# Four background tiles become six, loaded in halves, and side work is tied to its place in the list

## The chip, the cores and the metric

The kernel runs on one core of one Trainium2 chip (trn2). The metric is the device time of the program in microseconds (us), as the median of several runs; lower is better.

## The reference

A graph network of four layers on N = 2708 nodes with D = 512 features, all in float32. Only the first two layers matter here.

```python
deg = jnp.maximum((adj != 0).astype(jnp.float32).sum(-1), 1.0)
# layer 0
x = layernorm(x + (adj + head(adj)) @ x / rowsum(adj + head(adj)))
# layer 1: attention on the mask of adj, and a plain product with adj
h = x @ W_sa;  s_left = h @ a_sa[0, :512];  s_right = h @ a_sa[0, 512:]
e = where(adj != 0, exp(-leaky_relu(s_left[:, None] + s_right[None, :], 0.01)), 0)
x_a = (e / (sum(e, axis=1) + 1e-5)) @ h
x_b = adj @ (x @ W_gcnb) + b_gcnb
attn_a, attn_b = sigmoid([adj @ x, x] @ Wa.T + ba), sigmoid([adj @ x, x] @ Wb.T + bb)
x = layernorm(x + sigmoid(attn_a * x_a + attn_b * x_b))
# layer 2: three products with adj in a row; layer 3: adj + I, scaled by deg ** -0.5 on both sides
```

`deg`, the count of non-zero entries in each row, is used by the last layer.

## The kernel before

**Tiling.** The host hands in the transposed adjacency `adjT`. Nodes are split in two halves of NH = 1354, so `adjT` has four quarters, named 11, 12, 21 and 22. A product of adjacency and features is done by a scheme with seven instead of eight block products, P1 to P7. It needs sums and differences of the quarters: s1 = 21 + 22, s3 = 11 - 21, s2 = s1 - 11, s4 = 12 - s2. A `sweep` takes one range of output columns after the other; in each range the seven products run one after the other on TensorE (PE), each over ten tiles of 128 rows, and the rest of the rows (KR = 74 of each half) is added by small matmuls. [...]

**Stages.** `S` gives the start of each stage in units of one product of a sweep: S[0] = 0 is layer 0, S[1] = 28 a sweep with the plain adjacency over one range (1024, 330), S[2] = 35 the attention sweep over four ranges of 384, 384, 256 and 330 columns, SB = 63 the plain adjacency for the other 1024 columns by two nested levels of the scheme (`sweep2`), and S[3] to S[6] layers 2 and 3.

**Order.** Nothing is issued directly. `at(pos, fn, hold)` puts a piece of work into a list at a position in those units. The list is sorted, and the functions are called in its order. The framework then places the instructions on the engines by that order and by when they would be ready, so an instruction can be placed ahead of one that is earlier in the list if that one is not ready yet. With `hold=True` each instruction of the piece gets an ordering edge, without a semaphore, from the instruction ahead of it in the list on its engine: it can't be placed before that one. At run time every engine works in the order that was placed.

**Around the attention sweep.** In a range that starts at position pb, the tiles 11, 21, 22 and 12 of `adjT` come through SP's queue into a ring of 38 buffers. `prep2` (L1143 to L1145) makes each tile into e: two ACT operations (Prelu, Exp) and one on VectorE (DVE). `comb` (L407) makes the sums on DVE. `add_run` (L766 to L770) adds tiles up on DVE, and `run_sums` (matmul L783) turns the sum into row sums on PE, for h = 1 at pb + 4.7 and h = 0 at pb + 5.2. Their reciprocals `rd` (L1156, L1157) scale the output rows as these leave PSUM (`done2`, matmul L610, ACT L1198), from pb + 5.15 and pb + 7.12.

**Background.** During S[2], the sums s1 to s4 of the other 1024 columns are made and written to DRAM (`SD`, "As" in the profile) for SB, and their counts are taken for `deg`. There are two sets of 512 columns (`RANGES_B`), each with ten steps and a step for the rest of the rows. In a step, `back_load` loads four tiles of 128 x 512 (L1059, 256 KB each, on the GpSimd (POOL) queue); `back_tally` takes Sign twice and Square once per pair of tiles on ACT (L1072, L1073) and adds to `dg` on DVE (L1075); `back_sums` makes the four sums in place on DVE (L1095) and stores each (L1096, POOL queue). The four tiles `w_0` to `w_3` have one buffer each. After a set, `back_end` (matmul L1103) makes the degrees and `back_rows` stores them as a row.

**In S[1].** `score` (L907) takes dot products of each feature row with the attention vectors on DVE, `scores_end` collects them, and `score_rows` turns them over with PE (`to_rows`, L924) into a row in DRAM that S[2] reads. Two of the four products are taken for 16 of the tiles in S[2]. `pair` in `extra1` (ACT L973, L974; DVE L980) counts the columns of S[1]'s own range, and `end` there (L993) sums them on PE.

Of the kernel before, what the change touches and what calls it, by code (L numbers as in the profile page):

```python
# [21 lines left out]
F32 = mybir.dt.float32  # L22
# [3 lines left out]
P = 128  # L26
EPS = 1e-5
NH = 1354
# [43 lines left out]
def gnn_kernel(ctx: ExitStack, tc: tile.TileContext, x, adjT, w_sa, a_sa, w_gcn, b_gcn, wab, bab, w_hop, w_out,  # L72
# [873 lines left out]
    for R0, n in RANGES:  # L946
        full = R0 == RANGES_A[0][0]
        for h in (1, 0):
            ts = tiles_of(R0, n)
            for k in ts:  # L950
                p = S[1] + 0.55 + 0.21 * i
                at(p, lambda t=h * KT + k: get_x1(t))
                at(p + 0.25, lambda t=h * KT + k, w=wt(k), js=range(4 if full else 2): score(t, w, got1, js))
                i += 1
            at(p + 0.26, lambda a=(h * KT + ts[0], len(ts), False): scores_end(*a))
            if full:
                at(p + 0.26, lambda a=(h * KT + ts[0], len(ts), True): scores_end(*a))
            at(p + 0.8, lambda R0=R0, h=h, ts=ts: score_rows(R0, h, ts))
    at(p + 0.27, scores_over)
    for i, (h, k) in enumerate((h, k) for g in (4, 0) for h in (0, 1) for k in range(g, g + 4)):  # L960
        p = S[2] + 1.6 + 1.3 * i
        at(p, lambda t=h * KT + k: get_x1(t))
        at(p + 0.4, lambda t=h * KT + k: score(t, P, got1, (2, 3)))
        if k % 4 == 3:
            at(p + 0.41, lambda a=(h * KT + k - 3, 4, True): scores_end(*a))

    def extra1(pb, r, R0, n, A):
        ts = tiles_of(R0, n)

        def pair(keys, w=P):  # L970
            m = pool.tile([P, 2, D], BF, name="sg", tag="nat", bufs=6)
            for h, key in enumerate(keys):
                nc.scalar.activation(m[:w, h, :n], A[(r,) + key][:w, :n], AF.Sign)  # L973
            nc.scalar.activation(m[:w, :, :n], m[:w, :, :n], AF.Square)  # L974
            if R0 not in deg:
                deg[R0] = d = pool.tile([P, 2, D], BF, name="dg", tag="nat", bufs=6)
                nc.vector.tensor_copy(d[:w, :, :n], m[:w, :, :n])
            else:
                d = deg[R0]
                nc.vector.tensor_tensor(d[:w, :, :n], d[:w, :, :n], m[:w, :, :n], ALU.add)  # L980

        for k in range(KW):
            at(pb + 0.1 + 0.8 * k / KT, lambda k=k: pair((("11", k), ("21", k))))
            at(pb + 3.9 + 0.8 * k / KT, lambda k=k: pair((("12", k), ("22", k))))
        for key, w in (("r", KA), ("r32", 32)):
            at(pb + 4.8, lambda key=key, w=w: pair(((key, 0), (key, 1)), w))

        def end(h):
            d = deg[R0]
            ps = bank("ds", [P, 4])  # L990
            for i, q in enumerate(ts):
                wq = wt(q)
                nc.tensor.matmul(ps[:wq, i : i + 1], d[:, h, q * P - R0 : q * P - R0 + wq], ones_bf[:, 0:1], start=True,  # L993
                                 stop=True)
# [12 lines left out]
        at(pb + 5.9, lambda: rows(1))  # L1007
        at(pb + 5.2, lambda: end(0))
        at(pb + 5.9, lambda: rows(0))
# [37 lines left out]

    back = {}

    def back_tiles():  # L1050
        return [feat.tile([P, D], F32, name=f"bk_{c}", tag=f"w_{c}") for c in range(4)]

    QUARTERS = ((0, 0), (1, 0), (1, 1), (0, 1))

    def back_load(i0, k):
        back["t"] = ts = back_tiles()
        for t, (hi, hj) in zip(ts, QUARTERS):
            j0, c0 = hj * NH + k * P, hi * NH + i0
            nc.gpsimd.dma_start(out=t, in_=adjT[j0 : j0 + P, c0 : c0 + D])  # L1059

    def back_rest_load(i0):
        back["t"] = ts = back_tiles()
        for h in range(2):
            a = adjT[:, h * NH + i0 : h * NH + i0 + D]
            rows_over(nc.gpsimd, ts[h], (a[NH - KR : NH], a[2 * NH - KR :]))
            nc.gpsimd.dma_start(out=ts[2 + h][:32], in_=a[2 * NH - 32 :])

    def tally(pair, w):

        m = pool.tile([P, 2, D], BF, name="sg", tag="nat", bufs=6)  # L1070
        for h in range(2):
            nc.scalar.activation(m[:w, h, :], pair[h][:w], AF.Sign)  # L1072
        nc.scalar.activation(m[:w], m[:w], AF.Square)  # L1073
        d = back["d"]
        nc.vector.tensor_tensor(d[:w], d[:w], m[:w], ALU.add)  # L1075

    def back_start():
        back["d"] = pool.tile([P, 2, D], BF, name="dg", tag="nat", bufs=6)
        nc.gpsimd.memset(back["d"], 0.0)

    def back_tally():
        a11, a21, a22, a12 = back["t"]
        tally((a11, a21), P)
        tally((a12, a22), P)

    def back_rest_tally():
        ts = back["t"]
        tally(ts[:2], KA)
        tally(ts[2:], 32)

    def back_sums(i0, k):
        a11, a21, a22, a12 = back["t"]
        for m, o, a, b, op in (("s1", a22, a21, a22, ALU.add), ("s3", a21, a11, a21, ALU.subtract),
                               ("s2", a11, a22, a11, ALU.subtract), ("s4", a12, a12, a11, ALU.subtract)):
            nc.vector.tensor_tensor(o, a, b, op)  # L1095
            nc.gpsimd.dma_start(out=SD[m][k * P : (k + 1) * P, i0 : i0 + D], in_=o)  # L1096

    def back_end(i0):
        d = back.pop("d")
        ps = bank("ds", [P, 8])  # L1100
        for h in range(2):
            for i in range(4):
                nc.tensor.matmul(ps[:, 4 * h + i : 4 * h + i + 1], d[:, h, i * P : (i + 1) * P], ones_bf[:, 0:1], start=True,  # L1103
                                 stop=True)
# [8 lines left out]
        q = h * KT + i0 // P  # L1113
        to_rows(rdeg[:, q : q + 4], 4, DROW[h][0, i0 : i0 + D].rearrange("(k i) -> k i", i=P))

    p = S[2] + 1.3
    for i0, _ in RANGES_B:
        at(p, back_start)
        for k in range(KW):
            at(p, lambda i0=i0, k=k: back_load(i0, k))  # L1120
            at(p + 0.6, back_tally)
            at(p + 0.7, lambda i0=i0, k=k: back_sums(i0, k))
            p += 1.13
        at(p, lambda i0=i0: back_rest_load(i0))
        at(p + 0.6, back_rest_tally)
        at(p + 0.85, lambda i0=i0: back_end(i0))
        at(p + 0.9, lambda i0=i0: back_rows(i0, 0))
        at(p + 0.95, lambda i0=i0: back_rows(i0, 1))
        p += 1.13

    def start2b():
        W[2] = [spare_part(s, g) for s in ("T1", "T2", "T3", "T4") for g in "BD"]
# [14 lines left out]
    def extra2(pb, r, R0, n, A):  # L1147
        def rows(h):
            row[R0, h] = tmp("row")
            m = (n + P - 1) // P  # L1150
            src = SROW[R0, h][0:1, :]
            nc.sync.dma_start(out=row[R0, h][:, : m * P].rearrange("p (k i) -> p k i", i=P),
                              in_=bass.AP(tensor=src.tensor, offset=src.offset, ap=[[0, P], [P, m], [1, P]]))

        def share(o, s, t, w):
            nc.vector.tensor_scalar(o, s, 1e-5, None, ALU.add)  # L1156
            nc.vector.reciprocal(o, o)  # L1157
            if R0 == RANGES_A[0][0]:
                nc.vector.tensor_tensor(o, o, gate[:w, t, 0:1], ALU.mult)

        at(pb - 1.6, lambda: rows(0))
        at(pb - 1.0, lambda: rows(1))
        at(pb + 5.2, lambda: run_sums(R0, n, 0, share))
        at(pb + 4.7, lambda: run_sums(R0, n, 1, share))

    def finish_x2(y, x1, w, t, h, r0):

# [608 lines left out]
```

## Time and profile before

| | |
|---|---|
| median of 3 runs | 2927.16 us (2924.32 to 2930.38) |
| the profiled execution | 2930.68 us |
| its span, first to last instruction | 2928.9 us |
| mean granted TensorE clock | 0.988 |
| PE / DVE / ACT / POOL busy | 97% / 78% / 23% / 22% of the span |
| data moved | 554.41 MB, 189 GB/s |
| `bk<-in_adjT` loads (L1059) | 80 of 256 KB, 4.6 us from issue to landing (median) |
| `As<-bk` stores (L1096) | 80 of 256 KB, 3.2 us (median) |

PE is the TensorE matmul, PEld its weight loads, DVE VectorE, ACT ScalarE, POOL GpSimd, SP SyncE. A row such as `L1095 DVE bk<-bk,bk` names the line, the engine and what is written from what. In the list of waits, `PE rs L783 <- DVE run L770` says that PE stood idle ahead of the instruction of line 783 that writes rs, until DVE's instruction of line 770 that writes run had ended. The profile's windows give for a stretch of time the busy time of each engine with the count of instructions, then the granted clock of TensorE, the busy share of the DMA engines and GB/s.

### The profile page before, as it was taken

How to read it: one execution, taken by the hardware profiler on the slowest of the kernel's cores; microseconds unless marked ns; L12 is line 12 of the kernel's file. 1: busy time of each engine (PE TensorE's matmuls, PEld its weight loads, DVE VectorE, ACT ScalarE, POOL GpSimd, SP SyncE). 2: the span in 40 equal slices, each digit the busy share in tenths (PEclk: the TensorE clock that was granted, in tenths of full speed). 3: DMA queues.
4: the chain of work that ended last, by engine and by line, in shares of the span. 5: the costliest groups of instructions: out<-in, count | busy, mean ns of one | idle time of the engine just before them, and what ended most of it. 6: DMA issues, size and time to landing. Idle time of an engine off the chain costs nothing.

```text
span 2928.9 us, 38864 instructions
## 1 busy us (share of the span) xinstructions
PE 2832.2 (97%) x11159; PEld 1913.9 (65%) x11159; DVE 2292.8 (78%) x5890; ACT 661.3 (23%) x1314; POOL 650.8 (22%) x1175
## 2 busy tenths in 40 slices
PE   7999999999989899999999999999999999999998
PEld 5655666556576678777666666666666666656665
DVE  6898688676667657677599877987878877899986
ACT  4554214765557311201200000000000100100001
POOL 0123233222232210213202224021230221501102
PEclk9999999999999999999999999999999999999999
DMA  7666466466566565577767768566675565854652
GB/s 225 194 204 186 140 206 205 138 206 190 168 203 197 164 183 146 176 221 244 228 177 240 211 196 257 166 184 213 192 251 165 177 202 176 251 152 138 182 140 79
DMA packets 404959, 554.41 MB, mean 189 GB/s; under 512 B 68752, under 2 KB 350556, under 8 KB 404744
## 3 DMA queue, kind: packets, MB, share of 16 engines
q1 hardware_dynamic: 330976, 391.33, 45.8%
q0 software_dynamic: 56032, 148.83, 15.4%
q10 hardware_dynamic: 17736, 11.76, 1.4%
q8 instruction: 89, 1.46, 0.2%
q14 instruction: 126, 1.03, 0.1%
HBM read 468.02 MB, written 83.65 MB: 188 GB/s over the span
## 4 chain that ended last, share of the span: by engine, by line
PE 71%; DVE 12%; issue 6%; DMA 6%; POOL 3%; ACT 1%; SPq 1%; POOLq 0%; DVEq 0%; ACTq 0%
PE accd L1356 13%; PE accu L1356 13%; PE accc L1356 12%; PE ps_d L610 6%; PE acca L1356 6%; PE accd L462 4%; PE accc L462 3%; PE accr L1427 3%; PE accu L462 3%; DMA bk<-in_adjT 2%; PE acca L462 2%; DVE z L1301 2%; DMA As<-bk 1%; PE accr L1431 1%; PE ps L649 1%
## 5 line engine op out<-in xcount | busy, mean ns | idle before, releaser
L1301 DVE TENSOR_TENSOR z<-z 128x339 f32<-128x339 f32 (+2 forms) x1176 | 538.4, 490 | 20.4 <-PE accu L1356 10.6
L1374 ACT COPY q<-accu 128x339 f32<-128x339 f32 (+2 forms) x105 | 41.6, 429 | 1056.7 <-PE accu L1356 836.2
L1356 PE MATMUL accc<-s,t 128*128 128x339 f32 (+2 forms) x784 | 233.5, 439 | 0.2 <-DVE s L1301 0.2
L1356 PE MATMUL accu<-z,t 128*128 128x339 f32 (+2 forms) x784 | 227.7, 436 | 4.2 <-DVE z L1301 3.0
L1356 PE MATMUL accd<-z,t 128*128 128x339 f32 (+2 forms) x784 | 227.8, 436 | 1.7 <-DVE q L1438 1.4
L1356 PE MATMUL accc<-z,t 128*128 128x339 f32 (+2 forms) x784 | 226.8, 436 | 0.5 <-ACT q L1374 0.5
L564 POOL TENSOR_TENSOR rstd<-rstd,neg_half 128x1 f32<-128x1 f32 (+3 forms) x91 | 59.7, 656 | 702.0 <-DVE rstd L563 446.9
L1356 PEld LDWEIGHTS accu<-z,t 128*128 128x128 f32 x784 | 148.1, 190 | 70.1 <-DVE z L1301 6.1
L1356 PEld LDWEIGHTS accc<-s,t 128*128 128x128 f32 x784 | 146.8, 190 | 70.7 <-issue 10.2
L1356 PEld LDWEIGHTS accd<-z,t 128*128 128x128 f32 x784 | 148.1, 190 | 66.7 <-DVE q L1438 2.3
L1356 PEld LDWEIGHTS accc<-z,t 128*128 128x128 f32 x784 | 148.2, 190 | 64.8 <-ACT q L1374 1.0
L1380 DVE TENSOR_TENSOR q<-q,accd 128x338 f32<-128x338 f32 (+2 forms) x140 | 67.9, 485 | 148.3 <-PE accd L1356 148.0
L1301 DVE TENSOR_TENSOR s<-z 128x339 f32<-128x339 f32 (+2 forms) x392 | 178.0, 490 | 7.5 <-PE accc L1356 3.2
L1575 POOL DMA_DIRECT2D Y<-y x192 | 104.7, 552 | 330.0 <-DVE y L1570 289.2
L407 DVE TENSOR_TENSOR a<-a,a 128x384 f32<-128x384 f32 (+2 forms) x240 | 118.0, 516 | 5.3 <-DMA a<-in_adjT 4.3
L1143 ACT ACTIVATE e<-row,s_right 128x384 f32<-128x384 f32 (+5 forms) x176 | 94.8, 566 | 41.0 <-DVE a L1145 11.6
L1145 DVE SCALAR_TENSOR_TENSOR a<-a,e 128x384 f32<-128x384 f32 (+2 forms) x160 | 76.9, 508 | 34.1 <-ACT e L1144 34.0
L569 ACT ACTIVATE ld<-ld,rstd 128x512 f32<-128x512 f32 (+3 forms) x45 | 36.5, 813 | 263.9 <-DVE rstd L566 98.1
L1438 DVE TENSOR_TENSOR q<-q,accr 128x338 f32<-128x338 f32 (+2 forms) x160 | 69.1, 485 | 22.8 <-PE accr L1431 22.7
L1380 DVE TENSOR_TENSOR q<-q,accu 128x338 f32<-128x338 f32 (+2 forms) x175 | 79.2, 485 | 3.9 <-ACT q L1374 2.6
L774 DVE SCALAR_TENSOR_TENSOR s<-a,row 128x384 f32<-128x384 f32 (+2 forms) x152 | 75.3, 508 | 6.0 <-ACT row L759 6.0
L1144 ACT ACTIVATE e<-e 128x384 f32<-128x384 f32 (+5 forms) x176 | 78.9, 475 | 1.4
(699 smaller groups left out, 5907.5 us busy)
## 6 DMA issues: line engine op xcount, KB each, us to landing
z<-As SPq DMA_DIRECT2D x320, 169.5 KB
z<-As SPq DMA_DIRECT2D x320, 169.0 KB
z<-in_adjT SPq DMA_DIRECT2D x240, 169.5 KB
z<-in_adjT SPq DMA_DIRECT2D x240, 169.0 KB
a<-in_adjT SPq DMA_DIRECT2D x160, 192.0 KB
bk<-in_adjT POOLq DMA_DIRECT2D x80, 256.0 KB, 4.6
As<-bk POOLq DMA_DIRECT2D x80, 256.0 KB, 3.2
z<-As SPq DMA_DIRECT2D x160, 128.0 KB
```

The source lines that it names most:

```text
L407: nc.vector.tensor_tensor(A[r, dst, k][:, :n], A[r, a, k][:, :n], A[r, b, k][:, :n], op)
L462: nc.tensor.matmul(B[home, c][:, :n], X[STAT[p], k][:, c * P : (c + 1) * P], A[r, MOV[p], k][:, :n], start=bool(start and k == k0), stop=k ...
L610: nc.tensor.matmul(o, lhs(c), r, start=c == 0 and n == 0, stop=c == DC - 1, skip_group_check=True)
L774: nc.vector.scalar_tensor_tensor(t[:w, :n], a[:w, :n], 0.0, row[R0, h][:w, :n], ALU.is_gt, ALU.mult)
L1143: nc.scalar.activation(e[:w, :n], row[R0, h][:w, :n], AF.Prelu, bias=s_right[:w, t : t + 1], alpha=0.01)
L1144: nc.scalar.activation(e[:w, :n], e[:w, :n], AF.Exp, scale=-1.0)
L1145: nc.vector.scalar_tensor_tensor(a[:w, :n], a[:w, :n], 0.0, e[:w, :n], ALU.not_equal, ALU.mult)
L1301: nc.vector.tensor_tensor(d[:, :n], Z[x + (k,)][:, :n], Z[y + (k,)][:, :n], op)
L1356: nc.tensor.matmul(B[home][:, :n], stat(v, k), a[:, :n], start=bool(start and k == 0), stop=k == nk - 1, skip_group_check=True)
L1380: nc.vector.tensor_tensor(d[:, :n], s_[:, :n], B[home][:, :n], ALU.add)
L1427: nc.tensor.matmul(ps[r][:, :n], XA[:KA, c * P : (c + 1) * P], R[h, s][:KA, :n], start=True, stop=False, skip_group_check=True)
L1575: nc.gpsimd.dma_start(out=rows[:, :, f * P : (f + 1) * P], in_=o[32 * f : 32 * (f + 1), : m * P].rearrange("p (b d) -> p b d", d=P))
```

## The change

The background takes its tiles in turn from six buffers (the four `w_` tiles and the two of the pool tag `xT`) instead of four. A step's loads are split: 21 and 22 at 0.55 units ahead of the step's position p, 11 and 12 at p + 0.02. The steps begin at S[2] + 1.6 instead of 1.3 and are 1.12 units apart instead of 1.13. `back_sums` still makes s1, s3, s2 and s4 in this order. The end of a set moves from 0.85 to 1.4 units after its last load, its rows from 0.9 and 0.95 to 1.7 and 1.72, and `dg` is kept per set. `hold` is set for the tally, the sums, the end and the rows of the background, for `pair` in S[1], for the scores in S[2], for `score_rows` (moved from 0.8 to 1.5 units after its scores) and for `run_sums` of S[2] (h = 1 from 4.7 to 5.05, h = 0 from 5.2 to 6.5). The load of W[3] into the `w_` tiles moves from SB - 0.6 to SB - 0.2.

```diff
-            at(p + 0.8, lambda R0=R0, h=h, ts=ts: score_rows(R0, h, ts))
+            at(p + 1.5, lambda R0=R0, h=h, ts=ts: score_rows(R0, h, ts), True)
...
-        at(p + 0.4, lambda t=h * KT + k: score(t, P, got1, (2, 3)))
+        at(p + 0.4, lambda t=h * KT + k: score(t, P, got1, (2, 3)), True)
...
-            at(pb + 0.1 + 0.8 * k / KT, lambda k=k: pair((("11", k), ("21", k))))
-            at(pb + 3.9 + 0.8 * k / KT, lambda k=k: pair((("12", k), ("22", k))))
+            at(pb + 0.1 + 0.8 * k / KT, lambda k=k: pair((("11", k), ("21", k))), True)
+            at(pb + 3.9 + 0.8 * k / KT, lambda k=k: pair((("12", k), ("22", k))), True)
         for key, w in (("r", KA), ("r32", 32)):
-            at(pb + 4.8, lambda key=key, w=w: pair(((key, 0), (key, 1)), w))
+            at(pb + 4.8, lambda key=key, w=w: pair(((key, 0), (key, 1)), w), True)
...
-    def back_tiles():
-        return [feat.tile([P, D], F32, name=f"bk_{c}", tag=f"w_{c}") for c in range(4)]
-
-    QUARTERS = ((0, 0), (1, 0), (1, 1), (0, 1))
-
-    def back_load(i0, k):
-        back["t"] = ts = back_tiles()
-        for t, (hi, hj) in zip(ts, QUARTERS):
+    def back_tile(c):
+
+        i = back["i"] = (back.get("i", -1) + 1) % 6
+        if i < 4:
+            t = feat.tile([P, D], F32, name="bk", tag=f"w_{i}")
+        else:
+            t = pool.tile([P, DC, P], F32, name="bk", tag="xT", bufs=2).rearrange("p c i -> p (c i)")
+        back["next"][c] = t
+        return t
+
+    QUARTERS = ((1, 0), (1, 1), (0, 0), (0, 1))
+
+    def back_load(i0, k, half):
+        if not half:
+            back["next"] = {}
+        for hi, hj in QUARTERS[2:] if half else QUARTERS[:2]:
             j0, c0 = hj * NH + k * P, hi * NH + i0
-            nc.gpsimd.dma_start(out=t, in_=adjT[j0 : j0 + P, c0 : c0 + D])
+            nc.gpsimd.dma_start(out=back_tile((hi, hj)), in_=adjT[j0 : j0 + P, c0 : c0 + D])
+        if half:
+            back["t"] = back["next"]
...
     def back_sums(i0, k):
-        a11, a21, a22, a12 = back["t"]
+        a21, a22, a11, a12 = (back["t"][q] for q in QUARTERS)
...
-    p = S[2] + 1.3
+    p = S[2] + 1.6
     for i0, _ in RANGES_B:
-        at(p, back_start)
+        at(p, lambda i0=i0: back_start(i0))
         for k in range(KW):
-            at(p, lambda i0=i0, k=k: back_load(i0, k))
-            at(p + 0.6, back_tally)
-            at(p + 0.7, lambda i0=i0, k=k: back_sums(i0, k))
-            p += 1.13
+            at(p - 0.55, lambda i0=i0, k=k: back_load(i0, k, 0))
+            at(p + 0.02, lambda i0=i0, k=k: back_load(i0, k, 1))
+            at(p + 0.6, back_tally, True)
+            at(p + 0.7, lambda i0=i0, k=k: back_sums(i0, k), True)
+            p += 1.12
         at(p, lambda i0=i0: back_rest_load(i0))
-        at(p + 0.6, back_rest_tally)
-        at(p + 0.85, lambda i0=i0: back_end(i0))
-        at(p + 0.9, lambda i0=i0: back_rows(i0, 0))
-        at(p + 0.95, lambda i0=i0: back_rows(i0, 1))
-        p += 1.13
+        at(p + 0.6, back_rest_tally, True)
+        at(p + 1.4, lambda i0=i0: back_end(i0), True)
+        at(p + 1.7, lambda i0=i0: back_rows(i0, 0), True)
+        at(p + 1.72, lambda i0=i0: back_rows(i0, 1), True)
+        p += 1.12
...
-        at(pb + 5.2, lambda: run_sums(R0, n, 0, share))
-        at(pb + 4.7, lambda: run_sums(R0, n, 1, share))
+        at(pb + 6.5, lambda: run_sums(R0, n, 0, share), True)
+        at(pb + 5.05, lambda: run_sums(R0, n, 1, share), True)
...
-    at(SB - 0.6, startB3)
+    at(SB - 0.2, startB3)
```

More of the change, by code (lines that the diff above doesn't have):

```diff
@@ L1048, in gnn_kernel @@
     back = {}
-    def back_tiles():
-        return [feat.tile([P, D], F32, name=f"bk_{c}", tag=f"w_{c}") for c in range(4)]
-    QUARTERS = ((0, 0), (1, 0), (1, 1), (0, 1))
-    def back_load(i0, k):
-        back["t"] = ts = back_tiles()
-        for t, (hi, hj) in zip(ts, QUARTERS):
+    def back_tile(c):
[11 more added lines that the diff above has]
+        for hi, hj in QUARTERS[2:] if half else QUARTERS[:2]:
             j0, c0 = hj * NH + k * P, hi * NH + i0
-            nc.gpsimd.dma_start(out=t, in_=adjT[j0 : j0 + P, c0 : c0 + D])
+            nc.gpsimd.dma_start(out=back_tile((hi, hj)), in_=adjT[j0 : j0 + P, c0 : c0 + D])
+        if half:
+            back["t"] = back["next"]
     def back_rest_load(i0):
-        back["t"] = ts = back_tiles()
+        back["next"] = {}
         for h in range(2):
             a = adjT[:, h * NH + i0 : h * NH + i0 + D]
-            rows_over(nc.gpsimd, ts[h], (a[NH - KR : NH], a[2 * NH - KR :]))
-            nc.gpsimd.dma_start(out=ts[2 + h][:32], in_=a[2 * NH - 32 :])
+            rows_over(nc.gpsimd, back_tile((h, 0)), (a[NH - KR : NH], a[2 * NH - KR :]))
+            nc.gpsimd.dma_start(out=back_tile((h, 1))[:32], in_=a[2 * NH - 32 :])
+        back["t"] = back["next"]
     def tally(pair, w):
@@ L1073, in tally, with back_start @@
         nc.scalar.activation(m[:w], m[:w], AF.Square)
-        d = back["d"]
+        d = back["d"][back["i0"]]
         nc.vector.tensor_tensor(d[:w], d[:w], m[:w], ALU.add)
-    def back_start():
-        back["d"] = pool.tile([P, 2, D], BF, name="dg", tag="nat", bufs=6)
-        nc.gpsimd.memset(back["d"], 0.0)
+    def back_start(i0):
+        back["i0"] = i0
+        back.setdefault("d", {})[i0] = pool.tile([P, 2, D], BF, name="dg", tag="nat", bufs=6)
+        nc.gpsimd.memset(back["d"][i0], 0.0)
     def back_tally():
-        a11, a21, a22, a12 = back["t"]
-        tally((a11, a21), P)
-        tally((a12, a22), P)
+        t = back["t"]
+        for j in range(2):
+            tally([t[h, j] for h in range(2)], P)
     def back_rest_tally():
-        ts = back["t"]
-        tally(ts[:2], KA)
-        tally(ts[2:], 32)
+        t = back["t"]
+        for j, w in ((0, KA), (1, 32)):
+            tally([t[h, j] for h in range(2)], w)
     def back_sums(i0, k):
-        a11, a21, a22, a12 = back["t"]
+        a21, a22, a11, a12 = (back["t"][q] for q in QUARTERS)
         for m, o, a, b, op in (("s1", a22, a21, a22, ALU.add), ("s3", a21, a11, a21, ALU.subtract),
@@ L1098, in back_end @@
     def back_end(i0):
-        d = back.pop("d")
+        d = back["d"].pop(i0)
         ps = bank("ds", [P, 8])
```

## The prediction

> **What bounds the kernel now.** I read the page first, for who is busy.
>
> ```profile
> span 2928.9 us, 38864 instructions
> PE 2832.2 (97%) x11159; PEld 1913.9 (65%) x11159; DVE 2292.8 (78%) x5890; ACT 661.3 (23%) x1314; POOL 650.8 (22%) x1175
> ```
>
> PE is the bound: it is idle for 2928.9 - 2832.2 = 96.7 us in all. No DVE or ACT saving counts unless it closes a PE gap. So the second view is PE's waits in the stretch that the edits touch, 440 to 1020 us (columns: total us, times, longest):
>
> ```profile
> PE rs L783 <- DVE run L770: 21.1, 4, 8.7
> PE ds L1103 <- DVE dg L1075: 6.7, 1, 6.7
> PE ps_d L610 <- ACT sg L1073: 6.0, 1, 6.0
> PE ps_r L924 <- DVE s_left L918: 4.8, 2, 4.5
> PE ps_r L924 <- DVE s_right L919: 2.1, 1, 2.1
> PE ds L993 <- DVE dg L980: 0.4, 1, 0.4
> ```
>
> These six rows are 41.1 us, and with a 0.8 us wait of ps_d for DVE's W 41.9 us: nearly half of all PE idle time. rs is run_sums, L1103 back_end, L993 the counts of S[1], ps_r score_rows, sg the background's tally. Three rows (21.1 + 6.7 + 6.0) and the 0.8 lie in S[2], 34.6 us; the rest, 7.3 us, in S[1].
>
> Third, why DVE was late. The chain of waits (start, us, what) before the first rs gap:
>
> ```profile
> 601.39 6.00 DMA bk<-in_adjT
> 607.42 0.63 ACT sg L1072
> ...
> 611.30 0.70 DVE bk L1095
> 614.44 3.84 DMA As<-bk
> 618.57 5.90 DMA bk<-in_adjT
> 624.49 0.63 ACT sg L1072
> 625.38 1.07 ACT sg L1073
> 627.09 0.68 DVE bk L1095
> 628.58 1.87 DVE run L770 x4
> 630.50 1.04 PE rs L783 x6
> ```
>
> This is a closed loop: load, sign, combine, store, and only then the next load into the same tile, 618.57 - 601.39 = 17.2 us from load to load. The waits of ACT and of POOL between 560 and 990 us say the same:
>
> ```profile
> ACT sg L1072 <- DMA bk<-in_adjT: 70.0, 25, 8.6
> POOL bk L1059 <- DMA As<-bk: 65.1, 38, 4.7
> ```
>
> ACT stands 70.0 us in front of a background tile, with the exponentials of the attention queued behind it; DVE then waits for those (29.3 us for e) and for sg (30.2 + 27.6 us).
>
> Fourth, the price after a gap. Ten microseconds from each S[2] restart, three of the five (the number before the last two is the granted clock):
>
> ```profile
> 630.50:640.50 10.00, 10.00 (x35) 5.84 (x36) 8.51 (x27) 1.64 (x3) 2.27 (x5) 0.83 0.59 170
> 758.05:768.05 10.00, 10.00 (x31) 5.86 (x32) 8.31 (x23) 6.95 (x14) 0.62 (x2) 0.70 0.46 148
> 870.66:880.66 10.00, 10.00 (x39) 7.82 (x40) 6.73 (x22) 4.73 (x8) 1.62 (x3) 0.70 0.76 245
> ```
>
> PE is fully "busy" here but slow: 10 x (1 - clock) is 1.7, 3.0 and 3.0 us lost, and 1.8 and 2.2 us after the restarts at 914.18 and 984.90 (clocks 0.82, 0.78): 11.7 us. In S[1] the same sum after 469.51 and 514.13 (0.78, 0.83) is 3.9 us.
>
> **What the Trainium skill says.** "TensorE: Matmul & The Clock Gate", Part 1 (the HAM clock gate): an idle window of about 3.4 us drops PE to half rate until it has been busy again. The trace agrees: gaps of 4.3 to 8.7 us are followed by the clocks above. Same page, "Architectural detail": ACT and DVE queues are strict FIFO; that is why one late tile holds the exponentials. "DMA: Bandwidth & Descriptors", "Anatomy of one DMA": about 2.0 us fixed plus bytes / 436e3. For 256 KB this is an estimate of 2.6 us; the page of the profile has 4.6 us to landing for a load and 3.2 us for a store. The measured ones are used.
>
> **The change part by part.** One unit of the list is one PE step. From 576.7 us (36.0) to 1017 us (62.0) are 26 units, so 16.9 us per unit, and (440 - 46) / 26 = 15.1 us without gaps and half clock (34.6 + 11.7 = 46.3 us). In the 256-column range it is (106 - 18.5) / 7 = 12.5 us.
>
> *Work counts.* Nothing is added or removed. A background step keeps four Signs and two Squares on ACT (4 x 0.621 + 2 x 1.044 = 4.6 us), two dg and four bk operations on DVE (2 x 0.687 + 4 x 0.688 = 4.1 us) and eight DMA issues on POOL (8 x 0.54 = 4.3 us). DMA bytes are the same.
>
> *Six tiles, loads in halves.* The first pair of a step takes slots last used by the second pair two steps back, stored a whole period before (the two added slots, of xT, have no other user until after the last step): it is issued 0.55 before the step and has 1.15 units (17 us) until the tally. The second pair reuses the first pair of the step before, whose sums (s1, s3) now come first. The remaining loop is two sums 1.4 + store 3.2 + load 4.6 + tally 4.6 = 13.8 us, against a period of 1.12 x 15.1 = 16.9 us, or 14.0 us in the 256-column range. The old loop, 17.2 us, was no shorter than its period without gaps (1.13 x 15.1 = 17.1). So most of the 70.0 us of ACT waiting should go, ACT and DVE with it. The new wait, the second pair on POOL for a store, has behind it the next first pair, the As stores and the XB stores; POOL is busy 27% of 440 to 1020 us and XB's readers come much later, so it is covered; uncovered, it is the slower rival below.
>
> *run_sums.* h = 1 goes from 4.7 to 5.05 (0.35 units: 5.3 us, 4.4 in the narrow range), h = 0 from 5.2 to 6.5 (which had no gap). Gaps of 4.3, 6.0, 8.7 and 2.1 us: the first and last are covered by the shift alone, the second with any recovery of DVE. For the third, DVE stood 2.2 + 2.1 us for sg in the last 10 us before the run additions, which with the shift is 8.7: just closed, so I leave 2 us there. What is late next is rd for the drain at 5.15: rs now leads it by 0.1 units (1.5 us) instead of 0.45, and rs to rd has been two short DVE operations, under 1 us together where DVE is free.
>
> *back_end* goes from 0.85 to 1.4 after the last load, 0.55 units or 8 us, against the 6.7 us gap: gone. Two dg tiles now live at once for 0.28 units out of six "nat" buffers. The 6.0 us wait of ps_d goes with the late load at 905.9 that held ACT.
>
> So S[2] has 46.3 us to win; less 2 us kept in the narrow range, 2 us of clock there and 5 us for small new waits (a third of the background steps at 0.7 us, unseen in this trace; bounds 0 and 20): **37 us**.
>
> *score_rows* goes 0.7 units later (7 us in S[1]), pinned; pair is pinned. The ps_r gaps (6.9 us and 3.9 us of clock) lie ahead of PE steps whose other inputs come from DVE, which between 447 and 527 us is busy 73.0 of 80 us. The counts' ds already waits for dg at 519.24 and the gates for W at 519.9. A PE that arrives 10 us earlier waits there instead. Of 11.2 us I count **2 us**; bounds 0 and 9.
>
> *Scores of S[2] pinned; W[3] loaded at 62.8 instead of 62.4; background 0.3 later.* Nothing: a score is 4 x 0.5 us on a DVE that is idle 30% of the stretch; W[3] is four loads used at 65.6, 2.8 units later; if uncovered, one load of 5 us. Pins only forbid running early.
>
> Sum: 37 + 2 = 39 us. The profiled execution, 2930.68 us (span 2928.9), becomes 2892; the median of the runs is 3.5 us below it, so 2927.2 - 39 = **2888 us**.
>
> **Rivals.** *A: DVE is the bound in S[2] too.* As in S[1], the gaps come back at the next DVE-fed step. For it: DVE is busy 8.0 of 8 us in several stretches (832 to 856). Against: between 776 and 808 it is under half busy, ahead of PE. If two thirds of the S[2] gain go back and all of that in S[1], 37 / 3 = 12 us stay: 2915.
> *B: slower, by the pinned tally.* ACT and DVE can no longer start the background where it happens to be ready; if the second pair lands after its tally's place, ACT stands with the exponentials behind it, in every step. The loop (13.8) exceeds the period (14.0 at best in the narrow range) as soon as loads take their worst 6.0 us. It decides from 39 / 20 = 2 us of PE stall per step; at 3 us, half clock included, 20 x 3 - 39 = +21: 2948.
> *C: no difference.* The background ran at about its list places already, so pins hold nothing, and stores remain the limit: the rs gaps stay at 0.35 units' less, other waits take it: 2926.
>
> **How the numbers follow.** Forecast 0.67 (own range 2872 to 2908), A 0.16, C 0.04, B 0.13. The floor is 2927.2 - 57.5 (all of 46.3 + 11.2) = 2870; the range 2868 to 2922 holds the forecast and A, leaving out B and C, 0.17. A measurement can tell about 0.2%, 5.9 us: faster 0.67 + 0.16 = 0.83, same 0.04, slower 0.13.
>
> **What would show it.** Right: the wait of ACT's sg for bk under 20 us, PE's rs waits under 6 us, the L1103 gap gone, granted clock near 1 between 630 and 990 us; and in S[1] a longer ds or gates wait where ps_r waited. Wrong: sg still waiting for bk as long, or PE waiting for e-fed operations (a, s) in steps that had no wait.

## The result and the profile after

The changed kernel takes 2917.44 us (median of ten runs, 2914.74 to 2923.29) against 2928.65 us for the kernel before (ten runs, 2920.19 to 2932.97): a ratio of 0.9966, 95% interval 0.9955 to 0.9977. That is faster by about 10 us, where 39 us were forecast. 2917 is inside the range, close to what rival A gave (2915); whether A's mechanism was the reason is another matter, and the experiments say no.

The first lines of the page of the kernel after, to be set against those of before:

```profile
span 2913.0 us, 38876 instructions
PE 2824.2 (97%) x11159; PEld 1909.6 (66%) x11159; DVE 2293.2 (79%) x5890; ACT 662.2 (23%) x1314; POOL 650.6 (22%) x1175
```

PE is idle for 2913.0 - 2824.2 = 88.8 us instead of 96.7, and its busy time fell by 8.0 us for the same 11159 instructions. The span is 15.9 us shorter: half is idle time closed, half is a PE that was throttled less. (This execution is the fastest of its ten, 2.7 us under their median, and that of before was 2.0 us over its own, so the two traces show some 5 us more than the medians do.)

PE's waits of the kernel after between 440 and 1020 us (total us, times, longest):

```profile
PE ps_d L610 <- DVE C L523: 16.9, 4, 7.1
PE ds L993 <- DVE dg L980: 6.3, 1, 6.3
PE ps_d L610 <- DVE P1c L523: 5.9, 1, 5.9
PE ps_r L924 <- DVE s_left L918: 4.4, 1, 4.4
PE ps_n L593 <- DVE ld L829: 3.5, 1, 3.5
```

The 21.1 us for rs, the 6.7 us for back_end and the 6.0 us for ACT's sg are gone. In their place stand two new rows, C and P1c: L523 is the DVE addition that finishes a block of the result before its drain, the next thing in a range that DVE makes for PE. In S[2] PE now waits 16.9 + 5.9 = 22.8 us instead of 34.6. In S[1] it waits 6.3 + 4.4 = 10.7 us instead of 7.3. The last row, at the very start of S[1], isn't new: before it was 3.7 us, for P1c, and the prediction's list left it out.

The clock after the restarts at 640.3, 867.0, 902.5 and 975.3 us (it is the third figure from the end):

```profile
640.30:650.30 10.00, 9.96 (x40) 7.67 (x41) 7.01 (x19) 6.20 (x14) 1.09 (x2) 1.00 0.67 215
867.00:877.00 10.00, 9.99 (x37) 8.48 (x38) 2.94 (x7) 3.83 (x7) 2.66 (x5) 0.79 0.70 210
902.50:912.50 10.00, 10.00 (x38) 8.17 (x39) 7.60 (x18) 6.08 (x11) 2.14 (x5) 0.86 0.81 260
975.30:985.30 10.00, 9.96 (x31) 7.75 (x32) 7.24 (x25) 0.79 (x2) 0.00 (x0) 0.74 0.31 114
```

10 x (1 - clock) is 0, 2.1, 1.4 and 2.6 us: 6.1 us, where before lost 11.7. So S[2] gained 11.8 us of gaps and 5.6 us of clock, **17.4 us of the 37 forecast**.

Why so little: the waits of ACT, POOL and DVE between 560 and 990 us.

```profile
ACT sg L1083 <- DMA bk<-in_adjT: 65.9, 15, 12.8
POOL As L1108 <- DVE bk L1107: 143.2, 49, 22.3
POOL bk L1067 <- DMA As<-bk: 59.1, 36, 4.3
DVE dg L1086 <- ACT sg L1084: 58.9, 18, 15.2
DVE a L1158 <- ACT e L1157: 30.9, 19, 5.4
```

ACT still stands 65.9 us in front of a background tile (70.0 before), in fewer and longer waits: 15 instead of 25, the longest 12.8 instead of 8.6 us. POOL stands 143.2 us for sums whose stores it is to issue, with the next loads behind them in its queue. DVE waits 58.9 us for the count and 30.9 us for exponentials. The loop is still there. From the chain of waits that leads to the gap at 637.5 us (start, us, what):

```profile
602.74 5.47 DMA As<-bk
...
608.77 3.77 DMA bk<-in_adjT
...
612.57 1.15 ACT sg L1083 x2
...
618.21 0.68 DVE bk L1107
...
620.26 5.84 DMA As<-bk
...
626.67 4.14 DMA bk<-in_adjT
...
630.83 1.16 ACT sg L1083 x2
```

A store to DRAM must land (5.5 us) before the tile can be loaded again (3.8 us), then come the four Signs and two Squares (612.57 to 617.58), then the sums, and it begins again. Over the eighteen steps that follow another of their set, the median from a step's first sum to the landing of the last tile of the next step is 11.5 us, and from there to the next first sum 4.7 us. Before it was 14.6 and 1.7 us. So the tiles do come 3.1 us sooner, but from the last landing to the sums it has become 3.0 us longer: in the new order of the loads both pairs that are counted, 11 with 21 and 12 with 22, contain a tile of the late half, and s1 is written over 22, which must be counted first. Before, the count of 11 and 21 mostly began while 22 and 12 were under way. Steps follow each other every 16.7 us (median; 17.0 before).

These medians stand for a wide spread. Steps lie 11.8 to 30.0 us apart (12.5 to 29.8 before). In eleven of the eighteen the Signs waited for a tile; there it is 3.6 us from the last landing to the first sum, and 15.3 us from step to step (medians). In the other seven no Sign waited, and the steps lie 19.0 us apart. Before, Signs waited in fourteen of the eighteen, with 0.4 and 16.4 us.

### The profile page after: what moved, and what is told of

Same layout as the page of the kernel before. It is cut to its first block, busy times and chain, and to the rows that moved or that the text cites. A ratio compares the mean times of both kernels' runs of the same rounds, so it can differ in the third digit from the quotient of the medians.

```text
span 2913.0 us, 38876 instructions
## 1 busy us (share of the span) xinstructions
PE 2824.2 (97%) x11159; PEld 1909.6 (66%) x11159; DVE 2293.2 (79%) x5890; ACT 662.2 (23%) x1314; POOL 650.6 (22%) x1175
## 4 chain that ended last, share of the span: by engine, by line
PE 75%; DVE 10%; issue 5%; DMA 5%; POOL 2%; ACT 1%; SPq 1%; POOLq 0%; ACTq 0%; DVEq 0%
PE accd L1369 14%; PE accu L1369 13%; PE accc L1369 13%; PE ps_d L610 7%; PE acca L1369 6%; PE accu L462 4%; PE accd L462 4%; PE accr L1440 3%; PE accc L462 3%; PE acca L462 3%; DMA bk<-in_adjT 2%; DMA As<-bk 1%; DVE z L1314 1%; PE accr L1444 1%; PE ps L649 1%
## 5 line engine op out<-in xcount | busy, mean ns | idle before, releaser
L1158 DVE SCALAR_TENSOR_TENSOR a<-a,e 128x384 f32<-128x384 f32 (+2 forms) x160 | 78.4, 507 | 36.2 <-ACT e L1157 34.7
L1451 DVE TENSOR_TENSOR q<-q,accr 128x338 f32<-128x338 f32 (+2 forms) x160 | 69.1, 484 | 22.8 <-PE accr L1444 22.7
```

Source lines behind the costliest of these rows:

```text
L1158: nc.vector.scalar_tensor_tensor(a[:w, :n], a[:w, :n], 0.0, e[:w, :n], ALU.not_equal, ALU.mult)
```

## The experiments

Each kernel was timed against the kernel before on the same chip, in several rounds and not all on one chip, so across rows it is the ratios that compare. "Gaps" is PE's idle time for waits over 0.15 us between 560 and 1020 us in the profiled run, "ACT" the wait of the background's Signs for their tiles. (In order, run_back and stores_sp one such wait, of 10.5, 11.4 and 5.0 us, is named otherwise in the list of waits; a background tile landed less than 0.1 us ahead of its end, so it is counted here.) The intervals are 95%.

| kernel | median us | ratio to before | gaps | ACT |
|---|---|---|---|---|
| before | 2928.65 to 2931.78 | 1 | 34.6 | 70.0 |
| after | 2917.44 | 0.9966 (0.9955 to 0.9977) | 22.8 | 65.9 |
| tiles | 2914.57 | 0.9950 (0.9937 to 0.9962) | 20.3 | 47.2 |
| order | 2923.12 | 0.9974 (0.9963 to 0.9986) | 23.9 | 84.8 |
| s1_undone | 2916.53 | 0.9955 (0.9943 to 0.9967) | 22.1 | 66.7 |
| free_tally | 2894.23 | 0.9880 (0.9864 to 0.9896) | 4.6 | none |
| loose_back | 2915.68 | 0.9945 (0.9932 to 0.9957) | 16.8 | 49.8 |
| run_back | 2915.34 | 0.9949 (0.9938 to 0.9961) | 17.3 | 61.0 |
| loose_rb | 2920.24 | 0.9958 (0.9944 to 0.9971) | 21.3 | 55.7 |
| regroup | 2924.35 | 0.9976 (0.9966 to 0.9987) | 24.5 | 67.3 |
| pool_tally | 2979.50 | 1.0166 (1.0153 to 1.0179) | 52.8 | none |
| early_s1 | 2902.58 | 0.9899 (0.9883 to 0.9915) | 9.9 | 50.3 |
| stores_sp | 2902.56 | 0.9901 (0.9885 to 0.9918) | 11.8 | 49.7 |
| loose_sp | 2904.29 | 0.9907 (0.9893 to 0.9921) | 13.8 | 47.6 |
| before_sp | 2913.16 | 0.9942 (0.9927 to 0.9957) | 23.1 | 58.1 |
| tiles_sp | 2906.22 | 0.9921 (0.9907 to 0.9934) | 14.7 | 37.3 |
| early_sp | 2902.03 | 0.9910 (0.9894 to 0.9925) | 12.0 | 36.6 |

**The change in two halves.** tiles is the kernel before with only the six tiles and the split loads. order is the kernel after with four tiles and one burst of loads, so it has only the pins, the new positions and the new order of the loads.

```diff
  tiles (on before):
...
+            at(p - 0.55, lambda i0=i0, k=k: back_load(i0, k, 0))
+            at(p + 0.02, lambda i0=i0, k=k: back_load(i0, k, 1))
  order (on after):
-        i = back["i"] = (back.get("i", -1) + 1) % 6
+        i = back["i"] = (back.get("i", -1) + 1) % 4
-            at(p - 0.55, lambda i0=i0, k=k: back_load(i0, k, 0))
-            at(p + 0.02, lambda i0=i0, k=k: back_load(i0, k, 1))
+            at(p, lambda i0=i0, k=k: back_load(i0, k, 0))
+            at(p, lambda i0=i0, k=k: back_load(i0, k, 1))
```

> The kernel before with six background tiles and loads in halves alone: no pins, step positions 1.3 and 1.13, end of a set, run_sums and scores where they were. Theory L (the loop from store to load to tally stays, since the late pair still waits for the stores of the same step's first pair one step back): little change, 0 to 6 us faster than before; ACT still waits 55 us or more for bk, the rs waits stay at 12 us or more. Theory P (the tiles made the gain of the change): 9 to 12 us faster, rs waits under 8 us. Theory D (DVE has too much work ahead of the drain, whatever ACT waits for): 0 to 3 us.

> The changed kernel with four tiles, all loaded at p in one burst: pins and positions alone. Theory L: most of the gain of the change is here, 5 to 10 us faster than before, ACT's wait for bk 65 to 85 us, the rs waits gone, a wait of ps_d for C in their place. Theory P: within 4 us of before.

By the ratios the tiles alone give about 15 us, the rest alone about 8, both together no more than the tiles alone: the parts don't add up. PE and ACT in tiles, 560 to 990 us:

```profile
PE rs L783 <- DVE run L770: 7.7, 2, 6.6
PE ps_d L610 <- DVE C L523: 4.6, 2, 4.4
ACT sg L1083 <- DMA bk<-in_adjT: 47.2, 18, 9.2
```

Without any shift of run_sums the rs gaps are already 7.7 us instead of 21.1. Much of what the prediction had put down to the shift thus came with the tiles.

**The wait itself taken away.** free_tally is the kernel after, but the Signs read a row that is always in SBUF instead of the tile, so the counts for `deg` are not those of the adjacency. The number and size of the ACT and DVE operations stay.

```diff
-            nc.scalar.activation(m[:w, h, :], pair[h][:w], AF.Sign)
+            nc.scalar.activation(m[:w, h, :], vec[1][:w], AF.Sign)
```

> The changed kernel, but the background's Signs read a constant row (the bias) and not the tile, so the counts for deg are not those of adj; the work on every engine stays the same and only ACT's wait for the background loads is taken away. Theory L: ACT's wait for bk is 0, the waits of PE in S[2] fall from 22.8 us to under 8, 14 to 24 us faster than the changed kernel (ratio to before 0.988 to 0.992). Theory D: PE's waits for C and P1c stay above 15 us and the time is within 5 us of the changed kernel (0.995 to 0.998).

The time falls by 34.7 us from the kernel before, and PE in S[2] (560 to 990 us) is left with

```profile
PE ps_d L610 <- DVE C L523: 3.8, 1, 3.8
PE accd L462 <- DVE a L407: 0.8, 1, 0.8
```

DVE has all the work it had, and nearly all gaps are gone: the amount of DVE's work is not the bound in S[2] (rival A, theory D). What PE waited for hung on the Signs' wait for late tiles. The way from there to PE shows in DVE's waits in this run, 560 to 990 us:

```profile
DVE dg L1086 <- ACT sg L1084: 28.1, 8, 15.0
DVE a L1158 <- ACT e L1157: 28.1, 20, 5.4
```

The wait for exponentials hardly changes (30.9 us in after), the wait for the count is halved (58.9). So it is mainly in front of its own adds to the count that DVE stood, with products, runs and C behind them. How much each part of this is worth the run doesn't say: it also frees the sums of the Signs, which takes the tally out of the loop, and the framework places the work anew (about a quarter of DVE's instructions of S[2] stand elsewhere in its order than in after).

**S[1].** In s1_undone `score_rows` is back at 0.8 and `pair` loses its hold.

```diff
-            at(p + 1.5, lambda R0=R0, h=h, ts=ts: score_rows(R0, h, ts), True)
+            at(p + 0.8, lambda R0=R0, h=h, ts=ts: score_rows(R0, h, ts))
-            at(pb + 0.1 + 0.8 * k / KT, lambda k=k: pair((("11", k), ("21", k))), True)
+            at(pb + 0.1 + 0.8 * k / KT, lambda k=k: pair((("11", k), ("21", k))))
...
```

> The changed kernel with score_rows back at 0.8 units, and it and the pairs of S[1] without pins. Theory M (DVE bounds the end of S[1], so gaps only move): ps_r waits about 7 us and ds under 1 us as before, sum of the S[1] gaps between 6 and 11 us, and the time within 4 us of the changed kernel, rather faster than slower. Theory S (the S[1] edits are a gain): 5 to 10 us slower than the changed kernel.

The time is that of after within the error. In the trace ps_r then waits 5.1 + 1.9 us and ds 2.1 us, 9.1 us in all; with the edits it is 4.4 for ps_r and 6.3 for ds. The gap moves from one step that DVE feeds to the next.

**The pins and positions, taken out one at a time.** loose_back drops the hold of the background's tally and sums, run_back puts `run_sums` back at 5.2 and 4.7 without hold, loose_rb does both.

```diff
-            at(p + 0.6, back_tally, True)
-            at(p + 0.7, lambda i0=i0, k=k: back_sums(i0, k), True)
+            at(p + 0.6, back_tally)
+            at(p + 0.7, lambda i0=i0, k=k: back_sums(i0, k))
...
-        at(pb + 6.5, lambda: run_sums(R0, n, 0, share), True)
-        at(pb + 5.05, lambda: run_sums(R0, n, 1, share), True)
+        at(pb + 5.2, lambda: run_sums(R0, n, 0, share))
+        at(pb + 4.7, lambda: run_sums(R0, n, 1, share))
```

> The kernel after with hold taken from the background's tally and sums alone (back_tally, back_sums, back_rest_tally); six tiles, half loads and all positions and other pins stay. Open is what makes the tiles with pins worth less (about 11 us) than the tiles alone (about 14 us). If the pins of the tally cost it (theory H): the Signs are placed behind exponentials that are ready first, ACT's wait for bk falls from 66 to 50 us or less, the PE gap for C (16.9 us by the list) to under 9 us, and the time is 2908 to 2914 us. If the moved positions cost it (theory Q: run_sums at 5.05 and 6.5, steps 0.3 later), ACT's wait may fall but the time stays at 2915 to 2919 us. If loosening lets the tally run too late and the loop gets longer, 2920 us or more.

> The kernel after with run_sums of S[2] put back to 5.2 (h = 0) and 4.7 (h = 1), without hold; all else as after. The prediction took the shift for the end of the 12.6 us of gaps for rs. If the shift is a gain (theory R): rs gaps of 5 to 12 us come back ahead of L783, and the time is 2921 to 2927 us. If the gaps only move to the next step that DVE feeds (theory M2): the rs gaps come back, those for C shrink by as much, and the time stays within 3 us of 2917 us. If the shift costs (theory Q): the time is 2911 to 2914 us.

> The kernel after without hold on the background's tally and sums and with run_sums of S[2] at 5.2 and 4.7 without hold: both edits that alone came to 0.9945 and 0.9949 of before. If each took away a cost of its own (theory H + Q): the gains add up and the time is 0.992 to 0.9935 of before. If both only undo the same loss against the tiles alone (theory U: what is left is the tiles' gain): 0.994 to 0.9955 of before, and ACT's wait for bk about 47 us as with the tiles alone.

All three, after and tiles have intervals that overlap. Once the tiles are there, no pin and no shift has an effect that these runs can tell from none, and the two that looked like gains alone didn't add up in loose_rb (theory U). In loose_back ACT's wait fell to 49.8 us as theory H had it, but the time stayed above its 2908 to 2914 us. In run_back the rs gaps are back with 6.2 us, those for C fall from 16.9 to 8.0 and those for P1c from 5.9 to 3.1: in these traces the shift of run_sums chose which wait PE stands in (theory M2), and no gain of it shows.

**Shorter loops.** regroup loads 21 and 11 first, then 22 and 12, so that one pair could be counted early.

```diff
-    QUARTERS = ((1, 0), (1, 1), (0, 0), (0, 1))
+    QUARTERS = ((1, 0), (0, 0), (1, 1), (0, 1))
...
```

> The kernel after with the halves of a step grouped by pair: the first half loads 21 and 11, the second 22 and 12, so the first pair for the count is complete half a step early; the four sums and their order are unchanged. If the late second half is what ACT waits for (theory L): the first Sign and dg no longer wait, but the second pair's still do, and s1 can't be made earlier than before; ACT's wait for bk falls from 66 us by a quarter to a half, to 33 to 50 us, and the time by 2 to 6 us to 2911 to 2916 us. If only the arrival of a step's last tile counts, nothing changes: ACT's wait moves to the second pair, 60 us or more, 2916 to 2919 us.

Its time lies above both forecasts: 0.9976 against 0.9966 for after. The intervals overlap, so a loss isn't shown; a gain isn't either. ACT's wait stays (67.3 us): s1 is written over 22, which is now itself in the late half. early_s1 keeps the halves, and counts 21 and 22 and makes s1 before the second half is needed.

```diff
...
+            at(p + 0.025, first_signs, True)
+            at(p + 0.03, lambda i0=i0, k=k: first_sum(i0, k), True)
             at(p + 0.6, back_tally, True)
```

> The kernel after with each step's count and sums split: the Signs of 21 and 22, which the first half loads a step ahead, and the sum s1 with its store come at p + 0.025, before the second half is needed; the Signs of 11 and 12, the Squares, the adds to dg and the other three sums stay at p + 0.6. Work and transfers are the same; the loop loses what s1's tile waited for (Signs of late tiles before its store). If the loop of late tiles is the cost (theory L): one of the two tiles that the next second half needs is free half a step sooner, but the other still follows s3; only two Signs instead of four follow a late tile, ACT's wait for bk falls from 66 to 35 to 55 us, and the time by 3 to 8 us to 2909 to 2914 us. If s3's tile alone sets the loop: ACT's wait stays above 55 us, 2914 to 2919 us. If the further pinned pieces disturb the order of exponentials and products more than they help (as regroup did): 2920 us or more.

It gains more than expected, some 20 us on after by the ratios (15 by the medians, which come from different rounds), with the same work. DVE and PE of early_s1, 560 to 990 us:

```profile
DVE dg L1111 <- ACT sg L1110: 21.6, 12, 4.1
PE ps_d L610 <- DVE C L523: 8.4, 2, 4.3
PE rs L783 <- DVE run L770: 1.5, 1, 1.5
```

ACT's wait itself falls only to 50.3 us, no lower than in tiles (47.2); but its longest is 6.9 instead of 12.8 us, two Signs instead of four follow the late tile, and DVE's wait for the count falls from 58.9 us to 21.6 (its sums wait another 11.9 us for Signs, 2.3 in after). So ACT's total is a poor measure of the cost; what reaches DVE decides.

stores_sp moves only the queue that issues the stores of the sums.

```diff
-            nc.gpsimd.dma_start(out=SD[m][k * P : (k + 1) * P, i0 : i0 + D], in_=o)
+            nc.sync.dma_start(out=SD[m][k * P : (k + 1) * P, i0 : i0 + D], in_=o)
```

> The kernel after with the background's stores of the sums (As<-bk) issued by SP's queue instead of POOL's; loads, positions and pins as after. In after POOL waits 143 us for the sums before it issues stores, with the next step's loads queued behind. If that order on POOL is what makes the tiles late (theory O): the second half's loads go out 1 to 3 us sooner, ACT's wait for bk falls from 66 to under 45 us, and the time is 2903 to 2912 us. If the loop itself does (theory L: a tile can't be loaded before its sum is stored, whichever queue issues): the loads still follow the landing of s1 and s3, ACT's wait stays at 55 to 70 us and the time at 2914 to 2919 us. If SP's own loads of a, queued behind stores that wait for DVE, come late, DVE waits for a<-in_adjT and the time is above 2920 us.

PE and ACT of stores_sp, 560 to 990 us:

```profile
PE ps_d L610 <- DVE C L523: 8.8, 4, 6.9
ACT sg L1083 <- DMA bk<-in_adjT: 44.7, 12, 7.4
```

With the 5.0 us that the list names otherwise, the Signs wait 49.7 us, more than the 45 that theory O allowed; the time is as it said. From a step's first sum to the last load for the next step it takes 4.9 us (median; 5.9 in after), to its landing 10.1 us (11.5), and steps follow each other every 15.6 us instead of 16.7. Something that the change doesn't touch, the queue in which the stores stand, held the tiles as much as their number did. SP's loads of a, now behind the stores, cost nothing that shows.

loose_sp puts stores_sp on top of loose_rb. before_sp does the same edit to the kernel before, tiles_sp to tiles, early_sp to early_s1 (there s1's early store goes to SP too).

> The kernel after without hold on the background's tally and sums, run_sums at 5.2 and 4.7 without hold, and the stores of the sums on SP's queue: loose_rb and stores_sp together. If the stores' queue matters (theory O), it lies 5 us or more under loose_rb; if it doesn't (theory L), within 2 us of it.

> The kernel before, with its four tiles and one burst of loads, and only the stores of the background's sums moved from POOL's queue to SP's. If POOL's queue was what held the loads (theory O): ACT's wait for bk falls from 70 us to under 50 us and the time by 12 to 28 us, to 0.990 to 0.996 of before, as far as stores_sp came with six tiles. If the want of buffers holds them (theory B: with four tiles each load waits for its own tile's store whichever queue issues): ACT's wait stays at 60 to 75 us, 0.997 to 1.001 of before. If SP's loads of a, behind stores that wait for DVE, come late: over 1.002.

> The kernel before with the six tiles and half loads, without any pin or moved position, and the stores on SP's queue. If tiles and queue together are what counts (theories B and O) and pins and positions nothing: 0.9895 to 0.992 of before, as stores_sp with all pins (0.9901). If the pins and positions are needed once the stores are on SP: 0.993 or more.

> The kernel after with s1 and the Signs of its two tiles early (early_s1, 0.9899) and the stores on SP's queue (stores_sp, 0.9901). If both remove the same wait: 0.988 to 0.9905 of before, ACT's wait for bk 35 to 45 us. If they remove two different parts: ACT's wait under 30 us and 0.984 to 0.988; below about 0.987 there is little left, since the Signs without any wait for tiles gave 0.988.

loose_sp is 16 us under loose_rb: the queue matters (theory O). With the four old tiles it is worth 17 us by itself, more than the whole change, and the tiles add 7 us in tiles_sp: both theories, O and B, hold a part, and the parts overlap (ACT's 58.1 us in before_sp lies between their forecasts). early_sp is no faster than stores_sp or early_s1, so to judge by the time they remove the same wait. An edit of the queue also lets the framework place the work anew (about a tenth of DVE's instructions of S[2] stand elsewhere in stores_sp than in after), but the gain came on four of the five kernels that got it, 8 to 19 us by the ratios, so a lucky order is unlikely to be the reason.

**The wait moved to another engine.** pool_tally lets GpSimd count (one is_equal with 0 per tile), so that the late tile is awaited where no exponential is behind it.

```diff
-            nc.scalar.activation(m[:w, h, :], pair[h][:w], AF.Sign)
-        nc.scalar.activation(m[:w], m[:w], AF.Square)
+            nc.gpsimd.tensor_scalar(m[:w, h, :], pair[h][:w], 0.0, None, ALU.is_equal)
...
```

> The kernel after with the background's count taken by GpSimd instead of ACT: one is_equal with 0 per tile on POOL (80 full tiles and the rests) instead of two Signs and a Square per pair, and the degree as 2708 less the count of zeros. The wait for late tiles then stands on POOL's queue, where only the stores and the next loads are behind it, and no longer ahead of exponentials. If it is the place of the wait on ACT that costs (theory L): there is no ACT wait for bk, the gaps for C in S[2] go as they did when the Signs read a resident row (free_tally, 2894 us), and the time is 2893 to 2903 us, somewhat above that, since DVE still waits for late tiles. If a late tile costs wherever it is awaited (theory T: the sums and the add on DVE wait as long), the time is 2912 to 2919 us. If POOL's counting is slow enough to lengthen the loop (several us per tile), or slows DVE[...], DVE's waits grow and the time is above 2920 us.

It is the slowest of all, and the groups of its page point to the reason (operation, count, then busy us and mean ns, then idle us before it and the releaser):

```profile
L1083 POOL TENSOR_SCALAR sg<-bk 128x512 bf16<-128x512 f32 (+2 forms) x88 | 136.3, 1569 | 10.7 <-DMA bk<-in_adjT 9.3
L1085 DVE TENSOR_TENSOR dg<-dg,sg 128x1024 bf16<-128x1024 bf16 (+2 forms) x44 | 36.0, 818 | 122.3 <-POOL sg L1083 122.3
```

A tile takes 1.57 us to count instead of ACT's 0.62, four in a row are 6.3 us in the loop, and DVE waits 122.3 us for them. DVE's wait for exponentials fell to 18.8 us and PE's gaps still grew to 52.8 us: freeing the exponentials of the tiles didn't help while DVE stood for the count. The sums are made in place, so they need the count wherever it is made.

Eight tiles, two whole sets, weren't tried.

## Why the prediction was wrong in size

- **The step that failed** is "The remaining loop is two sums 1.4 + store 3.2 + load 4.6 + tally 4.6 = 13.8 us, against a period of 1.12 x 15.1 = 16.9 us". Both sides were mis-sized. From the first sum to the landing it reckons 1.4 + 3.2 + 4.6 = 9.2 us, and 11.5 were measured. Every part was longer than reckoned: by the medians of after, the second sum's store is issued 2.0 us after the first sum begins and takes 3.5 us, the last load is issued at 5.9 us and takes 5.1. (The stores of 5.5 and 5.8 us in the chain shown are slow ones.) The period was taken as even, and steps lie 11.8 to 30.0 us apart; the trace of before, with 12.5 to 29.8 us, could have shown that. So where steps bunch there is no slack, where 3.1 us were reckoned with: in eleven of eighteen the Signs still waited. That the tally came out as reckoned, 4.7 us in the median, is luck: the stretch from landing to first sum runs from 1.2 us, two Signs, to 17.1 us. The prediction also overlooked that before, less of the tally followed the last landing (1.7 us), and that the new grouping puts more of it there.
- **"So most of the 70.0 us of ACT waiting should go"** followed from it and fell with it: 65.9 us are left. The prediction named this as the sign that it would be wrong ("sg still waiting for bk as long"), and so it was.
- **The worth of that wait was about right.** 39 us were forecast, nearly all for an ACT free of late tiles; with the Signs freed in fact (free_tally) it was 34.7 us. That run takes away more than late tiles on ACT, as said above, so the agreement is in part luck.
- **run_sums.** The gaps for rs went, as said, but not their time. "What is late next is rd" was the wrong next step: it is C, and P1c, made by DVE behind the same late runs (run 636.31 to 639.82, C at 639.82, PE at 640.34 us). The 9 us that were left to S[2] (2 and 2 in the narrow range, 5 for "small new waits") were 22.8 us of gaps and 6.1 of clock. The runs show no gain of the shift (run_back).
- **back_end.** The 6.7 us gap is gone, and the 6.0 us wait for sg. The new position does the first: tiles, which lacks it, keeps 3.4 us of that gap, and order, which has it, none. The wait for sg is gone in both.
- **S[1].** That gaps would move to ds was right (0.4 to 6.3 us). The +2 us was not: 10.7 us of gaps and, from clocks 0.83 and 0.74, 4.3 us of half clock, against 7.3 and 3.9 before, so about 4 us lost in this trace. The bound of "0 and 9" excluded a loss without a reason. By the medians (s1_undone) it is too small to measure.
- **"Pins only forbid running early"**: nothing in the runs contradicts it, and no gain of the pins can be told once the tiles are there.
- **Rivals.** A gave the time (2915) and named the form, gaps that come back at the next step that DVE feeds, but its cause, DVE at its limit, is refuted by free_tally. B was right that the loop may not fit its period, and that loads can be late (it took 6.0 us as the worst; the trace of before already has one of 7.2). Yet PE's gaps per step fell from 1.7 to 1.1 us (34.6 and 22.8 over 20 steps) and didn't rise by the 2 us from which B decides. C is excluded by the interval.
- **The clock.** "TensorE: Matmul & The Clock Gate", Part 1, was used for the price of a gap: an idle window of some 3.4 us brings half rate. After agrees: the gap of 2.8 us before 640.3 is followed by a clock of 1.00, those of 5.0, 5.9 and 7.1 us by 0.74, 0.86 and 0.79. It is no sharp limit: in the trace of before a gap of 2.1 us, ahead of the restart at 514.13, was followed by 0.83, though the prediction speaks of gaps of 4.3 to 8.7 us only. Fewer long gaps gave 5.6 us of the 17.4.

What stays open: why pins and positions give about 8 us with four tiles (order) and nothing measurable with six; what in free_tally is due to ACT, to the shorter loop and to the new order of the work; and how much of the gain of stores_sp is POOL's order and how much a quicker transfer, since the trace shows no landing for the stores on SP.

## What to carry to other kernels

When work recycles its buffers, take the length of the loop from its own trace, from first sum to landed load, and not from a sum of medians, and set it against the shortest distance of two steps and not the mean: where steps bunch (here 11.8 us apart, with a mean of 17.4), a loop that fits on average is still waited for. Before adding buffers, look at what else stands in the queue that refills them, and at how much work must follow the last tile; here moving the stores to another queue (17 us) or doing one sum before the late half arrives (some 20 us on top of the change) was each worth about as much as the two buffers with their split loads (15 us). And when a wait is removed by a shift, ask what the same late engine makes next for the bound engine, for that is where the time goes.

## What the hardware showed that was not expected

- GpSimd took 1.57 us for is_equal over 128x512 float32 into bf16 (ACT's Sign: 0.62), and DVE's additions slowed beside it: dg<-dg,sg from 689 to 812 ns (both between 600 and 970 us). "SBUF — State Buffer", "Who interferes with whom", says that a DVE operation with two inputs in SBUF contends with a GpSimd operation that reads SBUF; the slower additions agree with it.
- In after, the later of a step's four stores take longer: from issue to landing 2.7, 3.3, 3.5 and 4.7 us in the order of issue (medians of 20 each, 256 KB).
- The time follows PE's gaps and not ACT's wait: ACT waits 47 to 50 us in tiles, early_s1 and stores_sp alike, while PE's gaps are 20.3, 9.9 and 11.8 us and the ratios 0.9950, 0.9899 and 0.9901.
